# A graph attention layer on one core: rows of x for 63 gather tiles fetched in the prologue, their k and v made in the walk

## The chip, the cores and the metric

The kernel runs on one core of a Trainium2 chip. Times are device microseconds (us) of one execution. The kernel before was timed nine times: median 2628.71 us, from 2615.65 to 2638.81. The profile is one execution, recorded by the hardware profiler; it took 2623.65 us.

The engines are named as in the profile: PE is TensorE (matmuls and transposes), DVE is VectorE, ACT is ScalarE, POOL is GpSimd, which here issues the indirect DMAs, and SP is SyncE, which issues nearly all other DMAs.

## The reference

There are 12500 nodes with 256 features, and 200000 edges (src, dst), sorted by dst. The layer first normalizes and clips, then attends over each node's incoming edges with 8 heads of 32, and then adds, normalizes and adds the input:

```python
h = relu(layernorm(x))
q, k, v = h @ Wq + bq, h @ Wk + bk, h @ Wv + bv          # each 12500 x 256, 8 heads of 32
logits  = sum over d of q[dst] * k[src] / sqrt(32)       # edge x head
attn    = softmax of logits over the edges of one dst
out     = sum over the edges of a dst of attn * v[src], + h @ Wskip + bskip
y       = h + gelu(out)
result  = x + layernorm(y) * gamma + beta
```

All of it is in 32-bit floating point.

## The kernel before, in words

**Prologue (0 to about 243 us).** `project` goes over x in 98 blocks of 128 rows: it loads them, makes the row statistics (DVE), normalizes and clips (ACT, L218), transposes twice (PE, L138), multiplies by the 256 x 512 matrix of Wk and Wv (PE, L247), adds the bias (DVE, L250) and stores h in the DRAM table `h_tab` and k and v, 512 numbers a node, in `kv_tab`. In between stands `make_plan`, which works out on the chip which edges and nodes belong to which step: it loads the edges' dst and src (`load_edges`, L390 and L392), stores them shifted (`dst_p`, `src_p`), cuts them into steps with 16 small indirect DMAs (L472), and writes tables: `idx` (the gathers' row numbers), `d0_row` (first node of each window), `pen_tab` (penalties for the running maxima), `e_tab` (six rows of numbers from which 0/1 matrices are made; L649, L658). The scheduler lays plan and projection into each other on DVE, PE and POOL; on POOL the plan alone stands. `pieces` splits a bias into three bf16 parts, so that a 3-row matmul can add it in PSUM.

**Walk (about 245 to 2590 us).** The edges are cut into 8 streams (S), each of 66 steps of up to 3 tiles (K) of 128 edges. A step handles one tile of all eight streams three times. For each tile, `gather` (L1024) issues eight indirect DMAs on POOL, one for a stream, each of 128 rows of 512 numbers from `kv_tab`, into one of six buffers `kv`. A buffer comes free when `weigh` of its tile is done; gathers for step c+2 are issued during step c. The rest of a tile:

- `spread` (PE, L1062): the rows of q for the edges, as a product of a 0/1 matrix `to_e` with the window of queries `qw`, in PSUM `ps_qe`, two halves.
- `times` (DVE, L1071, two halves): multiplies k by q in place; `total` (DVE, L1078) sums over a head.
- `weigh` (DVE, L1129): multiplies v by the weights, giving `vw`; `add_up` (PE, L1148) sums it over edges by the 0/1 matrix `to_n`. ACT copies the sums out, and the last node's sums into the next step's first tile (L1163).

Once a step: `maxima` (two scans on DVE, L1099 and L1100, a subtraction, and Exp on ACT, L1103), `turn_back` (PE, L1111), `hot_n` (PE and ACT, L1050 and L1052), and for step c+2 `turn_windows` (PE L1000, ACT L1003: 192 node rows `hw` transposed, in two parts), `queries` (PE L1013 and L1017, ACT L1019) and `hot_e` four times (PE L1039, ACT L1041).

**Pairs.** From step 10 on, finished nodes are closed in pairs of 128-row blocks: pair m is fetched in step 10 + 39m/32 and worked on in the two steps after it, so four steps in six both start on a new pair (`pair`) and end an old one (`before`), one has only an old one and one only a new one. `turn` and `skip` (PE L822, L835, L839), `divisors`, `divide` (DVE L814, L816, L828), `add` (PE L844), `gelu` (ACT), `stats` (DVE L851 to L857), `root` (ACT L861), and a step later `factors` (DVE L865, L866), `normal` (ACT L871), `shifted` (PE L878, L881), `scale` (DVE L885, L887) and `store` (SP).

**Order.** In the walk each instruction goes through `keep`, which fixes the order of every engine to that of the program text; so an instruction that waits holds up all that stands behind it on its engine. The loop's body (L1233 to L1333) is that order. Relevant places: `times` of the step's last tile opens the body and the `spread` for it closes the middle of the body before; between the last `hot_e` and that `spread` PE has nothing else:

```python
                for i in range(1, S // 2):
                    hot_e(c + 2, i)
            for half in range(2):
                times(c + 1, 1, half)
                if tiles_of(c + 1) == K:
                    spread(c + 1, K - 1, half)
```

Tiles live in pools with a number of buffers: `hw` 2, `pen` 2, `hT` and `o` of a pair 2, and PSUM `ps_hot` 2, shared by all of `turn_windows`, `queries`, `hot_e`, `hot_n`, `turn`, `shifted` and a part of `add_up`. When all buffers of a name are in use, the next writer waits for the last reader.

Of the kernel before, what the change touches and what calls it, by code (L numbers as in the profile page):

```python
# [57 lines left out]
SURE = 50  # L58
PAD = 127.0
# [8 lines left out]
def gnn_kernel(ctx: ExitStack, tc: tile.TileContext, x, src, dst, Wq, bq, Wk, bk, Wv, bv,  # L68
# [22 lines left out]
    w_q = consts.tile([P, KC, HID], F32, name="w_q")  # L91

# [3 lines left out]
    b_s3 = consts.tile([3, 2, HID], BF16, name="b_s3")  # L96
    nc.vector.memset(one_row, 1.0)
# [12 lines left out]
    def pieces(b3, b, scale):  # L110

        with tc.tile_pool(name="pcs", bufs=1) as pool:
            left = pool.tile([3, 3, HID], F32, name="left")
            t = pool.tile([3, 3, HID], BF16, name="piece")
            own = pool.tile([3, 2], F32, name="piece_of")
            nc.gpsimd.iota(own, pattern=[[1, 2]], base=0, channel_multiplier=1,
                           allow_small_or_imprecise_dtypes=True)
            rows(left[:, 0, :], b)
            nc.vector.tensor_scalar(left[:, 0, :], left[:, 0, :], scale, None, op0=OP.mult)
            for i in range(3):  # L120
                nc.vector.tensor_copy(t[:, i, :], left[:, i, :])
                if i < 2:
                    nc.vector.tensor_tensor(left[:, i + 1, :], left[:, i, :], t[:, i, :],
                                            op=OP.subtract)
            nc.vector.tensor_scalar(own[:, 1:2], own[:, 0:1], 0.0, None, op0=OP.is_equal)
            nc.vector.tensor_scalar(left[:, 0, :], t[:, 0, :], own[:, 1:2], None, op0=OP.mult)
            for i in (1, 2):
                nc.vector.tensor_scalar(own[:, 1:2], own[:, 0:1], float(i), None,
                                        op0=OP.is_equal)
                nc.vector.scalar_tensor_tensor(left[:, 0, :], t[:, i, :], own[:, 1:2],  # L130
                                               left[:, 0, :], op0=OP.mult, op1=OP.add)
            for i in range(2):
                nc.vector.tensor_copy(b3[:, i, :], left[:, 0, :])
# [20 lines left out]
    def project():  # L154
# [12 lines left out]
        with tc.tile_pool(name="proj_c", bufs=1) as cpool, \  # L167
# [18 lines left out]
            w_kv = cpool.tile([P, KC, 2 * HID], F32, name="w_kv")  # L186
# [36 lines left out]
            for g, (b0, n) in enumerate(zip(starts, sizes)):  # L223

                if g > 1 and g + 1 < len(sizes):
                    ready[g + 1] = prepare(g + 1)
                if g == 4:
                    make_near(tc, near, near_n, lambda ins: behind(ins, last))
                if g == 3:
                    for ins in [rows(gam, gamma)] + \  # L230
                            [weights(t, w) for t, w in ((w_q, Wq), (w_s, Wskip))]:
                        behind(ins, products[-1])
                    qscale = 1.0 / math.sqrt(D)
                    nc.vector.tensor_scalar(w_q, w_q, qscale, None, op0=OP.mult)
                    pieces(b_q3, bq, qscale)
                    pieces(b_s3, bskip, 1.0)
                    pieces(b_o3, beta, 1.0)
                    zero = cpool.tile([WN, HID], F32, name="zero")
                    nc.vector.memset(zero, 0.0)
                    behind(nc.scalar.dma_start(h_tab[NP:, :], zero), products[-1])  # L240
                h = ready.pop(g)
                kvo = pool.tile([P, 6, KV], F32, name="kvo")[:, :n, :]
                for b in range(n):
                    hT, turned = transposed(pool, psum, h[:, b, :])
                    ps_kv = psum.tile([P, 2 * HID], F32, name="ps_kv", bufs=4)
                    for c in range(KC):
                        ins = nc.tensor.matmul(ps_kv, hT[:, c, :], w_kv[:, c, :], start=c == 0,  # L247
                                               stop=c == KC - 1)
                    products.append(ins)
                    nc.vector.tensor_tensor(kvo[:, b, :], ps_kv, b_kv, op=OP.add)  # L250
                for tab, t in ((h_tab, h), (kv_tab, kvo)):
                    nc.sync.dma_start(tab[b0 * P:(b0 + n) * P, :]
                                      .rearrange("(p b) d -> p b d", p=P), t)
                if g < 2:
                    ready[g + 1] = prepare(g + 1)
# [68 lines left out]
    pen_tab = dram.tile([NST, 2, S, CH + 1], F32, name="pen_tab")  # L324
    with tc.tile_pool(name="pln", bufs=1) as pool, tc.tile_pool(name="pln_e", bufs=1) as ep, \
            tc.tile_pool(name="pln_ps", bufs=1, space=PSUM) as psum:
        products = project()
        make_plan(tc, pool, ep, psum, src, dst, N, LEN, NST, SLACK, NT, dram, ident, flag,
                  idx, d0_row, slot_row, e_tab, pen_tab, products)
    fits = nc.values_load(flag[0:1, 0:1], min_val=0, max_val=1)  # L330
    many = nc.values_load(flag[0:1, 2:3], min_val=0, max_val=1)
    with tc.If(fits > 0) as branch:
# [3 lines left out]
                     gam, eps)  # L336
# [45 lines left out]
def load_edges(nc, pool, a, E, C, fill, name):  # L382
# [5 lines left out]
    for lo, hi in ((0, full // 16 * 16), (full // 16 * 16, full)):  # L388
        if lo < hi:
            nc.gpsimd.dma_start(t[lo:hi], a[lo * C:hi * C].rearrange("(p c) -> p c", c=C))  # L390
# [14 lines left out]

def make_plan(tc, pool, ep, psum, src, dst, N, LEN, NST, SLACK, NT, dram, ident, flag, idx, d0_row,
              slot_row, e_tab, pen_tab, products):
# [13 lines left out]
    nc.vector.memset(zero, 0)  # L421
    dst_i = load_edges(nc, ep, dst, E, C, N, "edges_i")
    nxt_i = load_next(nc, ep, dst, E, C, N)
    nc.gpsimd.dma_start(dst_p[0:1, :], zero)
    nc.gpsimd.dma_start(dst_p[1:, 0].rearrange("(p c) -> p c", c=C), dst_i)
    d = ep.tile([P, C + 1], F32, name="chk_d")
# [4 lines left out]
    src_i = load_edges(nc, ep, src, E, C, 0, "edges_i")  # L431
# [4 lines left out]
    hd = ep.tile([NST, S - 1, SLACK + 1], I32, name="hd")  # L436
    ld = ep.tile([NST, 1], I32, name="ld")
    nc.gpsimd.dma_start(hd, bass.AP(tensor=dst.tensor, offset=dst.offset + LEN - 1,
                                  ap=[[0, NST], [LEN, S - 1], [1, SLACK + 1]]))
    nc.gpsimd.dma_start(ld, bass.AP(tensor=dst.tensor, offset=dst.offset + E - 1,  # L440
                                  ap=[[0, NST], [1, 1]]))
# [28 lines left out]
    for t, tab in ((dch, dst_p), (sch, src_p)):  # L470
        for s in range(S):
            nc.gpsimd.indirect_dma_start(  # L472
                out=t[:, s, :CH], out_offset=None, in_=tab[:, :],
                in_offset=bass.IndirectOffsetOnAxis(ap=at_i[:, s:s + 1], axis=0))
    sf = pool.tile([NST, S, CH + 1], F32, name="sf")
# [174 lines left out]

    row(5, lambda t: nc.vector.tensor_tensor(t, dl, turn[:, :, None].to_broadcast([NST, S, CH]),
# [3 lines left out]
    ones = pool.tile([NST, S, CH], BF16, name="row_ones")  # L655
    nc.gpsimd.memset(ones, 1.0)
    for r in (3, 4):
        nc.gpsimd.dma_start(e_tab[:, r * S:(r + 1) * S, :], ones)  # L658
# [92 lines left out]
def walk_streams(tc, N, HID, NST, KL, many, ident, idx, d0_row, slot_row, near, near_n, e_tab, pen_tab, h_tab,  # L751
                 kv_tab, table, x, out, w_q, w_s, one_row, b_q3, b_s3, b_o3, gam, eps):
# [31 lines left out]
    class Pair:  # L784
# [7 lines left out]
        def places(self):  # L792
# [3 lines left out]
            self.o = self.pool.tile([P, 2, HID], F32, name="o")  # L796
# [3 lines left out]
            self.y = self.o  # L800
# [17 lines left out]
        def turn(self):  # L818
# [5 lines left out]
            self.hT = self.pool.tile([P, 2, KC, P], F32, name="hT")  # L824
            self.keep(nc.scalar.copy(self.hT, ps))  # L825

        def divide(self):
            self.keep(nc.vector.tensor_mul(  # L828
# [65 lines left out]
    class Last(Pair):  # L894
# [7 lines left out]
        def places(self):  # L902
# [5 lines left out]
            self.o = self.g = self.sums[:, :, HEADS:]  # L908
            self.y = self.x

# [15 lines left out]
    with ExitStack() as es:  # L926
# [51 lines left out]
        def penalties(c):  # L978

            g = step[c]  # L980
            g["pen"] = early.tile([P, CH + 1], F32, name="pen", bufs=2)
# [4 lines left out]
        def windows(c):  # L986

            hw = step[c]["hw"] = hold.tile([P, 3, HID], F32, name="hw")
# [32 lines left out]
        def gather(c, j):  # L1021
            t = gath.tile([P, S, KV], F32, name="kv")
            for s in range(S):
# [5 lines left out]
        def gather_next(c, j):  # L1029

            if c + 2 < NST and j < tiles_of(c + 2):
                gather(c + 2, j)

# [148 lines left out]
        penalties(1)  # L1182
        for c in range(2):
            for j in range(tiles_of(c)):
                gather(c, j)
            if c == 0:
                windows(1)
                prefetch(2)
        for i in range(S // 2):
            hot_e(0, i)  # L1190
        for c in range(2):
            for part in range(2):
                turn_windows(c, part)
                queries(c, part)
            if c == 0:
                windows(2)
# [36 lines left out]
        for c in range(NST - 1):  # L1233
# [8 lines left out]
            if c + 3 < NST:  # L1242
                windows(c + 3)
# [8 lines left out]
            if before:  # L1252
                before.factors()
                before.normal()
            if c + 2 < NST:
# [15 lines left out]
            if pair:  # L1271
                pair.turn()
                pair.divisors()
                pair.skip()
            for half in range(2):
# [5 lines left out]
            if pair:  # L1281
                table_of(AF.Gelu)
                pair.divide()
            if pair_next:
                pair_next.fetch()
            if before:
                before.store(1)
# [10 lines left out]
            if c + 2 < NST:  # L1298
# [3 lines left out]
                for i in range(1, S // 2):  # L1302
                    hot_e(c + 2, i)
            for half in range(2):
# [8 lines left out]
            if c + 2 < NST:  # L1313
                penalties(c + 2)
            if c + 3 < NST:
                prefetch(c + 3)
            if c == NST - 2:
# [3 lines left out]
                if pair_next:  # L1321
                    pair_next.turn()
                    pair_next.skip()
            if pair:
                table_of(AF.Sqrt)
                pair.stats()
                pair.root()
                table_of(AF.Exp)
# [436 lines left out]
```

## Time and profile before

| | |
|---|---|
| median of nine runs | 2628.71 us (2615.65 to 2638.81) |
| profiled execution: its time, its span | 2623.65 us, 2621.8 us |
| PE, DVE, ACT, POOL busy | 1969.8, 1920.3, 1080.0, 1842.4 us |
| mean granted PE clock | 0.831 of full speed |
| gathers L1024 | 1576, mean 1140 ns, from 245.6 to 2532.8 us |
| the walk, a step | 34.4 us without pairs (steps 0 to 9), 35.1 us on average with them |
| DMA moved | 597.84 MB, 228 GB/s |

How to read what follows: a row of the group list names the source line, the engine, the operation, the tiles it writes and reads, and how often; after the bar come the busy time and mean of one, and then the time that the engine idled just before these instructions and what ended it. "issue" is time in which nothing that the profile shows was waited for. A row of the list of waits gives the engine, the tile and line that waited, what it waited for, the sum in us, how often, and the longest. A row of a timeline gives the start and length in us and, in brackets, the idle time before it and its end. The clock is the share of TensorE's full speed that the chip granted.

### The profile page before, as it was taken

What the parts mean: (1) busy time and instruction counts of PE and PEld (TensorE: products, weight loads), DVE (VectorE), ACT (ScalarE), POOL (GpSimd) and SP (SyncE); (2) the same over time, 40 slices, a digit from 0 to 9 for tenths busy, and PEclk for the clock granted to TensorE, in tenths of its full rate; (3) what the DMA queues carried; (4) which work ended last, traced back from release to release, by engine and by line L of the source; (5) the groups of instructions that cost most, each with busy time, mean ns of one, the idle gap of its engine ahead of it and who ended that gap; (6) DMA issues with size and microseconds to landing.
All of it is one profiled execution on the core that took longest, in us unless ns stands there. A gap on an engine that the chain in (4) does not pass through costs nothing. (4 is left out here: it accounts for less than half of the span.)

```text
span 2621.8 us, 34668 instructions
## 1 busy us (share of the span) xinstructions
PE 1969.8 (75%) x10196; PEld 1140.2 (43%) x10196; DVE 1920.3 (73%) x2205; ACT 1080.0 (41%) x2583; POOL 1842.4 (70%) x1648
## 2 busy tenths in 40 slices
PE   7898666666777777777777777777777777777775
PEld 3443433333444444444444444444444444444443
DVE  8886766666777678777677777776877776867774
ACT  3431222233444444344354344444443444453433
POOL 2302777777777777777777777777777777777750
PEclk9998766777798888888788788888888788888877
DMA  7857777777787777877787787777777877777761
GB/s 276 292 229 231 227 208 209 214 220 219 237 242 227 227 236 234 238 236 229 224 242 232 233 245 232 234 240 217 238 244 226 243 239 218 239 229 226 225 210 50
DMA packets 275980, 597.84 MB, mean 228 GB/s; under 512 B 52295, under 2 KB 166164, under 8 KB 273600
## 3 DMA queue, kind: packets, MB, share of 16 engines
q0 software_dynamic: 128768, 423.23, 54.9%
q1 hardware_dynamic: 146482, 171.81, 20.0%
q8 instruction: 84, 1.38, 0.2%
q14 instruction: 116, 0.95, 0.1%
q10 hardware_dynamic: 530, 0.47, 0.1%
HBM read 512.83 MB, written 82.47 MB: 227 GB/s over the span
## 5 line engine op out<-in xcount | busy, mean ns | idle before, releaser
L1024 POOL DMA_INDIRECT kv<-kv_tab,idx x1576 | 1797.2, 1140 | 501.6 <-issue 450.7
L1071 DVE TENSOR_TENSOR kv<-ps_qe,kv 128x1024 f32<-128x1024 f32 x394 | 470.4, 1220 | 336.1 <-DMA kv<-kv_tab,idx 224.8
L1062 PE MATMUL ps_qe<-qw,to_e 64*128 64x256 f32 x3152 | 476.2, 438 | 127.1 <-DVE kv L1071 126.2
L1062 PEld LDWEIGHTS ps_qe<-qw,to_e 64*128 64x128 f32 x3152 | 339.1, 213 | 275.9 <-issue 138.7
L1078 DVE TENSOR_REDUCE L<-kv 128x64 f32<-128x2048 f32 x197 | 450.4, 2286 | 6.7
L1129 DVE TENSOR_TENSOR vw<-w,kv 128x2048 f32<-128x2048 f32 x197 | 450.1, 2285 | 5.6 <-ACT w L1114 5.6
L1148 PE MATMUL ps_a<-vw,to_n 128*32 128x264 f32 (+1 forms) x2344 | 258.0, 454 | 130.2 <-DVE vw L1129 109.9
L1019 ACT COPY qw<-ps_hot 128x256 f32<-128x256 f32 (+1 forms) x132 | 63.2, 479 | 654.7 <-PE ps_hot L1017 643.3
L1017 PE MATMUL ps_hot<-w_q,hwT 128*128 128x256 f32 x792 | 255.9, 469 | 1.0 <-ACT hwT L1003 0.8
L887 DVE TENSOR_TENSOR o<-sums,ps_hot 128x512 f32<-128x512 f32 x46 | 31.6, 688 | 268.8 <-PE ps_hot L881 268.5
L1017 PEld LDWEIGHTS ps_hot<-w_q,hwT 128*128 128x128 f32 x792 | 169.1, 229 | 85.2 <-issue 56.2
L1148 PEld LDWEIGHTS ps_a<-vw,to_n 128*32 128x32 f32 (+1 forms) x2344 | 99.9, 132 | 244.2 <-DVE vw L1129 142.8
L247 PE MATMUL ps_kv<-w_kv,hT 128*128 128x512 f32 x392 | 186.8, 620 | 21.5 <-ACT hT L140 20.5
L1003 ACT COPY hwT<-ps_hot 128x256 f32<-128x256 f32 (+1 forms) x132 | 62.3, 472 | 296.4 <-PE ps_hot L1000 290.5
L960 ACT ACT_TABLE_LOAD x138 | 177.1, 1283 | 2.4
L1148 PE MATMUL ps_hot<-vw,to_n 128*64 128x264 f32 x808 | 167.3, 574 | 2.3 <-DVE o L887 2.3
L1163 ACT COPY kv<-ps_a 1x264 f32<-1x264 f32 x388 | 142.9, 368 | 6.3
L1041 ACT ACTIVATE to_e<-ps_hot,ones 128x384 f32<-128x384 f32 x264 | 142.3, 582 | 6.9 <-PE ps_hot L1039 6.8
L844 PE MATMUL ps_a<-o,ident 128*128 128x256 f32 x184 | 73.7, 539 | 94.0 <-DVE o L828 94.0
L839 PE MATMUL ps_a<-w_s,hT 128*128 128x256 f32 x368 | 127.4, 506 | 12.6 <-ACT hT L825 9.6
L871 ACT ACTIVATE sums<-sums,nm,rstd 128x256 f32<-128x256 f32 x92 | 50.2, 593 | 207.0 <-DVE nm L866 207.0
L1039 PE MATMUL ps_hot<-et,near 48*128 48x384 bf16 x264 | 89.6, 340 | 42.3 <-ACT qw L1019 26.1
(282 smaller groups left out, 2195.7 us busy)
## 6 DMA issues: line engine op xcount, KB each, us to landing
kv<-kv_tab,idx POOLq DMA_INDIRECT x1576
kv_tab<-kvo SPq DMA_DIRECT2D x14, 1536.0 KB
hw<-h_tab SPq DMA_DIRECT2D x264, 64.0 KB
table<-sums_w SPq DMA_DIRECT2D x264, 61.9 KB
pen<-pen_tab SPq DMA_DIRECT2D x66, 192.5 KB
sums<-table SPq DMA_DIRECT2D x92, 132.0 KB
x_f<-in_x_dram SPq DMA_DIRECT2D x92, 128.0 KB
h<-h_tab SPq DMA_DIRECT2D x92, 128.0 KB
```

Source lines behind the costliest of these rows:

```text
L247: ins = nc.tensor.matmul(ps_kv, hT[:, c, :], w_kv[:, c, :], start=c == 0, stop=c == KC - 1)
L839: self.keep(nc.tensor.matmul(self.ps[:, b, :], self.hT[:, b, c, :], w_s[:, c, :], start=False, stop=False, skip_group_check=True))
L960: keep(nc.scalar.activation(dummy[:, 1:2], dummy[:, 0:1], function))
L1017: keep(nc.tensor.matmul(ps[:, b, :], g["hwT"][:, b, k, :], w_q[:, k, :], start=False, stop=k == KC - 1, skip_group_check=True))
L1024: nc.gpsimd.indirect_dma_start(out=t[:, s, :], out_offset=None, in_=kv_tab[:, :], in_offset=bass.IndirectOffsetOnAxis(ap=idx[:, s, j, c:c ...
L1041: keep(nc.scalar.activation(step[c]["to_e"][:, i, :], ps[:, :CH], AF.Relu, scale=-1.0, bias=ones))
L1062: keep(nc.tensor.matmul(ps[:, b, a, :], g["to_e"][r, 2 * half + a, j * P:(j + 1) * P], g["qw"][r, (half + a) * half, :], start=True, stop= ...
L1071: keep(nc.vector.tensor_tensor(k, g["qe", half].rearrange("p b a d -> p a b d"), k, op=OP.mult))
L1078: keep(nc.vector.tensor_reduce(g["L"][:, j, :].rearrange("p (s h) -> p s h", s=S), g["kv"][j][:, :, :HID].rearrange("p s (h d) -> p s h d" ...
L1129: keep(nc.vector.tensor_tensor(t[:, :, HEADS:].rearrange("p s (h d) -> p s h d", h=HEADS), wj[:, :, :, None].to_broadcast([P, S, HEADS, D] ...
L1148: keep(nc.tensor.matmul(ps[at:at + w, :], g["to_n"][:, j, i * P + at:i * P + at + w], g["vw"][j][:, s, :], start=j == 0, stop=j == tiles_o ...
L1163: keep(nc.scalar.copy(step[c + 1]["kv"][0][0:1, s, HID - HEADS:], ps[at:at + 1, :]))
```

## The change

The walk no longer gathers k and v for stream 0 in the last tile of steps 2 to 64 (63 tiles, `EARLY = 2`). Instead

- the prologue gathers, on POOL, the 128 x 256 rows of x of these edges' src nodes, three tiles to a buffer and three buffers, and SP stores them in order in a DRAM table `x_early`. The first 30 (`FIRST`) stand ahead of the load of the src edges, the other 33 behind the plan's 16 indirect DMAs. The loads `hd` and `ld` stand earlier, and the two constant rows of `e_tab` are written later, from the buffers of the other rows;
- the walk loads such a tile a few steps ahead (`early_fetch`, SP), makes its statistics (`early_stats`, DVE; `early_root`, ACT; `early_normal`, DVE and ACT), transposes it (`early_turn`, PE and ACT) and multiplies it by the weights of k and v with their bias (`early_project`, PE), from where ACT copies the result to the place in `kv` where the gather would have put it. `early_project` stands between the last `hot_e` and the `spread` of the step's last tile. The weights `w_kv` stay in SBUF for the walk, and the bias is split by two more `pieces`. Table loads for Sqrt and Exp now stand in every step that has such a tile, not only in those with a pair;
- for room in SBUF, `pen`, `hw`, `hT` and `o` have one buffer in the walk; so the penalties of step c+1 (instead of c+2) are loaded late in step c, the windows of step c+3 at the end of step c instead of at its start, the result of a pair is written over its x rows (`y` is `x`), and the second store of a pair stands before the next pair's fetch.

```diff
@@ project, gnn_kernel
+    w_kv = consts.tile([P, KC, 2 * HID], F32, name="w_kv")
+    b_kv3 = consts.tile([3, 2, HID], BF16, name="b_kv3")
...
+                    pieces(b_kv3, bk, 1.0, range(1))
+                    pieces(b_kv3, bv, 1.0, range(1, 2))
...
+                if g == 2:
+                    between(lambda ins: behind(ins, products[-1]))
@@ new
+def gather_early(nc, pool, x, at, x_early):
+    n, _, HID = x_early.shape
+    G = 3
+    gathers = []
+    for e in range(0, n, G):
+        m = min(G, n - e)
+        t = pool.tile([P, G, HID], F32, name="x_e", bufs=3)
+        for i in range(m):
+            gathers.append(nc.gpsimd.indirect_dma_start(
+                out=t[:, i, :], out_offset=None, in_=x[:, :],
+                in_offset=bass.IndirectOffsetOnAxis(ap=at[:, e + i:e + i + 1], axis=0)))
+        nc.sync.dma_start(x_early[e:e + m].rearrange("e p d -> p e d"), t[:, :m, :])
+    return gathers
@@ make_plan
+    hd = ep.tile([NST, S - 1, SLACK + 1], I32, name="hd")
...
+    gathers = early()
+    behind(gathers[0], ins)
...
-    src_i = load_edges(nc, ep, src, E, C, 0, "edges_i")
+    src_i = load_edges(nc, ep, src, E, C, 0, "edges_i", lambda ins: behind(ins, gathers[FIRST - 1]))
...
+    behind(gathers[FIRST], ins)
...
+    ones = pool.tile([NST, S, CH], BF16, name="row5", bufs=2)
+    nc.gpsimd.memset(ones, 1.0)
+    for r in (3, 4):
+        nc.gpsimd.dma_start(e_tab[:, r * S:(r + 1) * S, :], ones)
     row(5, lambda t: nc.vector.tensor_tensor(t, dl, turn[:, :, None].to_broadcast([NST, S, CH]),
@@ Pair
-            self.y = self.o
+            self.y = self.x
...
-            self.hT = self.pool.tile([P, 2, KC, P], F32, name="hT")
+            self.hT = self.pool.tile([P, 2, KC, P], F32, name="hT", bufs=1)
...
+            self.o = self.pool.tile([P, 2, HID], F32, name="o", bufs=1)
@@ walk_streams
-            g["pen"] = early.tile([P, CH + 1], F32, name="pen", bufs=2)
+            g["pen"] = early.tile([P, CH + 1], F32, name="pen", bufs=1)
...
-            hw = step[c]["hw"] = hold.tile([P, 3, HID], F32, name="hw")
+            hw = step[c]["hw"] = hold.tile([P, 3, HID], F32, name="hw", bufs=1)
...
-            for s in range(S):
+            for s in range(1 if is_early(c) and j == K - 1 else 0, S):
...
+        def is_early(c):
+            return EARLY <= c < NST - 1
+        def early_fetch(c):
+            if is_early(c):
+                step[c]["xe"] = hold.tile([P, HID], F32, name="xe")
+                keep(nc.sync.dma_start(step[c]["xe"], x_early[c - EARLY]))
+        def early_stats(c):
...
+            keep(nc.vector.bn_stats(st, g["xe"]))
+            keep(nc.vector.bn_aggr(g["mv"], st))
+        def early_root(c):
+            g = step[c]
+            keep(nc.scalar.activation(g["rs"][:, 0:1], g["mv"][:, 1:2], AF.Sqrt, bias=eps))
+        def early_normal(c):
+            g = step[c]
+            keep(nc.vector.reciprocal(g["rs"][:, 0:1], g["rs"][:, 0:1]))
+            keep(nc.vector.scalar_tensor_tensor(g["rs"][:, 1:2], g["mv"][:, 0:1], -1.0,
+                                                g["rs"][:, 0:1], op0=OP.mult, op1=OP.mult))
+            keep(nc.scalar.activation(g["xe"], g["xe"], AF.Relu, scale=g["rs"][:, 0:1],
+                                      bias=g["rs"][:, 1:2]))
+        def early_turn(c):
+            g = step[c]
+            ps = hot_ps.tile([P, 2, KC, P], F32, name="ps_hot")[:, 0]
+            for k in range(KC):
+                keep(nc.tensor.transpose(ps[:, k, :], g["xe"][:, k * P:(k + 1) * P], ident))
+            g["xT"] = hold.tile([P, KC, P], F32, name="xT_e", bufs=1)
+            keep(nc.scalar.copy(g["xT"], ps))
+        def early_project(c):
+            g = step[c]
+            ps = hot_ps.tile([P, 2 * HID], F32, name="ps_hot")
+            keep(nc.tensor.matmul(ps, one_row, b_kv3.rearrange("o b d -> o (b d)"), start=True,
+                                  stop=False, skip_group_check=True))
+            for k in range(KC):
+                keep(nc.tensor.matmul(ps, g["xT"][:, k, :], w_kv[:, k, :], start=False,
+                                      stop=k == KC - 1, skip_group_check=True))
+            keep(nc.scalar.copy(g["kv"][K - 1][:, 0, :], ps))
@@ the loop's body
-            if c + 3 < NST:
-                windows(c + 3)
             for half in range(2):
                 times(c, K - 1, half)
...
+            if is_early(c + 1):
+                early_normal(c + 1)
             if c + 2 < NST:
                 turn_windows(c + 2, 0)
...
                 pair.skip()
+            if is_early(c + 1):
+                early_turn(c + 1)
             for half in range(2):
                 times(c + 1, 0, half)
...
+            if before:
+                before.store(1)
             if pair_next:
                 pair_next.fetch()
-            if before:
-                before.store(1)
...
                     hot_e(c + 2, i)
+            if is_early(c + 1):
+                early_project(c + 1)
             for half in range(2):
                 times(c + 1, 1, half)
...
-            if c + 2 < NST:
-                penalties(c + 2)
+            penalties(c + 1)
             if c + 3 < NST:
                 prefetch(c + 3)
+                windows(c + 3)
+            early_fetch(c + 3)
...
+            if pair or is_early(c + 2):
+                table_of(AF.Sqrt)
             if pair:
-                table_of(AF.Sqrt)
                 pair.stats()
+            if is_early(c + 2):
+                early_stats(c + 2)
+            if pair:
                 pair.root()
+            if is_early(c + 2):
+                early_root(c + 2)
+            if pair or is_early(c + 2):
                 table_of(AF.Exp)
```

## The prediction

> **What bounds the kernel now.** The page first. GpSimd (POOL) is busy 70% of the span, and nearly all of it is one row, the gathers, whose idle time is almost only "issue", 0.30 us each:
>
> ```profile
> PE 1969.8 (75%) x10196; PEld 1140.2 (43%) x10196; DVE 1920.3 (73%) x2205; ACT 1080.0 (41%) x2583; POOL 1842.4 (70%) x1648
> L1024 POOL DMA_INDIRECT kv<-kv_tab,idx x1576 | 1797.2, 1140 | 501.6 <-issue 450.7
> L887 DVE TENSOR_TENSOR o<-sums,ps_hot 128x512 f32<-128x512 f32 x46 | 31.6, 688 | 268.8 <-PE ps_hot L881 268.5
> ```
>
> So POOL issues almost back to back from 245.6 to 2532.8 us. Does it set the time all along? VectorE's waits say. First the steps without pairs (282.5 to 625.6 us), then one full step of the pair phase (1713.4 to 1750.8), then another (1398.6 to 1432.1):
>
> ```profile
> DVE kv L1071 <- DMA kv<-kv_tab,idx: 110.3, 32, 6.6
> ...
> DVE o L887 <- PE ps_hot L881: 5.8, 1, 5.8
> DVE kv L1071 <- PE ps_qe L1062: 4.4, 1, 4.4
> ...
> DVE o L887 <- PE ps_hot L881: 6.1, 1, 6.1
> DVE kv L1071 <- PE ps_qe L1062: 0.3, 1, 0.3
> ```
>
> Without pairs VectorE waits only for gathered rows, 11 us of each 34.4 us step: POOL bounds. In full steps it waits for no gather at all: the loop runs through VectorE (28 us busy), the ACT and TensorE chain to L887 (5.8) and the q rows of the step's last tile, made by `spread` (0.3 or 4.4). I call a step with a new and an old pair F (37.4 or 33.5 us here), one with the old pair only E (30.2 at 1825.8), one with the new only B (31.9 at 1856.0). What makes the two F differ is TensorE's clock, seen in its timeline:
>
> ```profile
> 1725.33 2.00 PE L1062 MATMUL ps_qe<-qw,to_e 64*128 64x256 f32 x16
> 1730.98 2.08 PE L844 MATMUL ps_a<-o,ident 128*128 128x256 f32 x4 [3.66 <-DVE o L828]
> 1737.63 3.69 PE L1017 MATMUL ps_hot<-w_q,hwT 128*128 128x256 f32 x8
> 1742.47 0.32 PE L1039 MATMUL ps_hot<-et,near 48*128 48x384 bf16 x1 [0.16 <-ACT to_e L1041]
> 1742.48 1.82 PE L1062 MATMUL ps_qe<-qw,to_e 64*128 64x256 f32 x14
> ```
>
> ```profile
> 1416.40 1.13 PE L844 MATMUL ps_a<-o,ident 128*128 128x256 f32 x4 [1.25 <-DVE o L828]
> 1420.62 1.99 PE L1017 MATMUL ps_hot<-w_q,hwT 128*128 128x256 f32 x8
> 1423.77 0.32 PE L1039 MATMUL ps_hot<-et,near 48*128 48x384 bf16 x1 [0.16 <-ACT to_e L1041]
> 1423.78 2.04 PE L1062 MATMUL ps_qe<-qw,to_e 64*128 64x256 f32 x16
> ```
>
> After an idle gap of 3.66 us before L844 the matmuls run at half speed (L1017 x8: 3.69 us) and spread comes late; after 1.25 us they don't (1.99). In both, spread starts the moment the last `hot_e` is done: nothing waits in between.
>
> Third, how far POOL lags in cycles of six steps (four F, E, B), the first mixed, the second all slow; and three neighbouring gathers:
>
> ```profile
> 695.90:905.20 209.30, 153.59 (x888) 92.78 (x884) 158.11 (x157) 94.63 (x223) 165.41 (x145) 0.86 0.79 235
> 1676.10:1887.90 211.80, 164.08 (x888) 98.41 (x884) 157.80 (x158) 94.80 (x223) 164.68 (x146) 0.83 0.79 233
> ```
>
> ```profile
> 1714.30 0.96 POOL L1024 DMA_INDIRECT kv<-kv_tab,idx  x1 [0.30 <-issue]
> 1715.56 1.76 POOL L1024 DMA_INDIRECT kv<-kv_tab,idx  x1 [0.30 <-issue]
> 1717.63 0.95 POOL L1024 DMA_INDIRECT kv<-kv_tab,idx  x1 [0.30 <-issue]
> ```
>
> The columns are window, length, then busy time of TensorE, its weight load, VectorE, ScalarE and POOL, the clock, DMA share and GB/s. In the mixed cycle VectorE waits 13.5 us for gathers, so its chain alone is 196 us; in the slow cycle 0.5 us: chain 211.3, and POOL itself waits some 3 us. An undisturbed gather starts every 1.256 us; the stretched ones (232, 290 us in all) mostly end 0.83 us after a `weigh` (188) or the gamma multiply L885 (44).
>
> **The change, part by part.** The sum is made against the profiled execution, 2623.65 us (span 2621.8), 5.06 below the median of the nine runs.
>
> *63 gathers leave the walk.* Those stretches belong to VectorE instructions whose number stays, so a gather is worth 1.256 us: 79 us if POOL bounded everywhere. It does in steps 0 to 11: 12 x 1.256 = 15 us gained there (VectorE's additional 0.9 us a step lies in its 11 us wait).
>
> The Trainium skill, "SBUF — State Buffer", section "Who interferes with whom", has VectorE instructions with two SBUF operands share a port with GpSimd, yet says its probe saw no stall of descriptor generation. Here 188 of 197 weighs stretch a gather; by the page's probe the stretch would be the gathers' own, at 1.457 us each (mean plus issue), and the full gain 92 instead of 79 us.
>
> *The prologue takes them.* 63 x 1.256 = 79 us more on POOL, which is busy 45 of 245 us there. The first 30 (37.7 us) stand ahead of the src edge load (72.4 us, after 16.8 us idle), the other 33 (41.4 us) ahead of the d_d store (123.7). In the built order the plan's later pieces sit 9 to 10 projected blocks further back (gvu behind 65 blocks instead of 56, wide behind 70 instead of 60), at 2.217 us a block some 20 to 22 us; POOL arrives at them 27 to 29 us later by my count, so TensorE and VectorE wait some 7 us. The last e_tab row moves from behind 93 blocks to behind 98, the last: 6.5 us of plan after the projection's end. Sum +14. Ends: +6 (tail alone) and +30 (POOL's whole delay shows). Two more `pieces` and hd, ld earlier lie under the projection.
>
> *early_project before spread.* Bias matmul 0.38 (the row of L835's kind), two 128x512 products 1.85 (L247: four records of 0.46 at full clock), and some 0.55 until the PSUM buffer that hot_e just filled is free: 2.8 us between the last hot_e and spread, where today nothing waits. In F and B all of it is VectorE's; in E spread has some 1.8 us in hand, so 1.0. The ACT copy to kv (0.60) runs beside spread. The new bn_stats and bn_aggr (0.42 + 0.17) lie in the wait for spread.
>
> *early_normal, early_turn.* The Relu (0.59, as L218) stands on ACT between the pair's normal and the window copy, on the chain to exp and L887: +0.55 in F, +0.2 in E. The two small VectorE instructions (0.16 each) end before ACT reaches exp. The two transposes (0.45) delay spread of tile 1, in B about 0.4, and shorten the gap before L844 from 3.65 to 3.2 us. That remains slow: gaps of 3.24 us (at 714.8 and 994.7) were followed by half clock too.
>
> The Trainium skill, "TensorE: Matmul & The Clock Gate", Part 1, puts the drop to half rate behind an idle window of about 3.4 us. By that 3.2 us could keep the clock full, and the slow steps would gain their 4 us back; no row decides between 1.55 (full) and 3.24 before L844.
>
> *Single buffers.* hw: its load is issued after turn_windows' second part (1736.45), eight issues take about 4.9 us (0.6 each, an estimate from POOL's plain stores, L425), the rows are used at 1748.66; the cover is some 5 us, and if that went, TensorE would wait at most 4.9 + 2. pen: free after the scans (1716), used at 1750.8. y in x's tile: SP's next fetch waits for store(1), some 3 us (d_d's store took 3.3 to land, L503's wait), with hw's load behind it; still before 1736. hT and o are used once a step. Zero for these; the end is 2 us a step. Table loads of Sqrt and Exp come in every step now, on ACT after the last to_e, where it idles 7 us. SP issues 63 loads more; hidden.
>
> *Sum.* F +3.35 (2.8 + 0.55), E +1.2, B +3.3: 4 x 3.35 + 4.5 = 17.9 a cycle. Mixed: chain 196 + 17.9 = 213.9 against 209.5 now (POOL alone would be near 202): +0.7 a step. Slow: 211.8 + 17.9 = 229.7: +3.0 a step. 33 mixed steps (12 to 39, 46 to 50) +23; 18 slow ones (40 to 45, 51 to 62) +54; step 63 +3.4. In all 2623.65 - 15 + 14 + 80 = 2703 for an execution like the profiled one, and 2708 for a median like the one shown.
>
> **The rivals.** (1) POOL bounds after all: 2623.65 - 79 + 14 = 2559. It takes added chain below 7 us a cycle, thus slack of over 2 us before spread, and no slow cycle; against it, the 0.16 us gap in both timelines. The mixed cycles break even at 13.5 us, 2.5 per F. (2) The clock stays full, the gap being shorter: F 33.2 + 3.35, E 31.4, B 30 to 35, a cycle 207.6 to 212.6, 34.6 to 35.4 a step against 35.1, over 54 steps -27 to +16: 2596 to 2639. For it the fast F steps, against it that no two stand side by side. This and (1) are the other side. (3) The slow clock locks everywhere, as in 12 of 12 F steps of the slow cycles: 33 mixed steps at 38.3 instead of 35 cost 110 instead of 23: 2789. (4) Only the prologue as I fear: +30 instead of 14, 2718.
>
> **How the numbers follow.** The mixture with its bounds (prologue +6 to +30, single buffers to 2 us in some steps, half the PSUM wait) 2645 to 2765: 0.55, with (4) in it; (3) 0.17; (2) 0.16; (1) 0.12. I take 2708; 80% from 2600 to 2790, which leaves out (1) and the top of (3); the likeliest alone 2645 to 2765. 0.3% (8 us) is about what can be told from no change. Faster: (1) and most of (2), 0.22; same 0.04; slower 0.74.
>
> **What would show it.** Early steps at 33.1 us instead of 34.4; the first walk gather near 260; in F a wait of VectorE for spread of 3 to 7 us, no wait for gathers; early_project's matmuls directly ahead of spread; POOL waiting for buffers, thus idle beyond "issue". Wrong if VectorE still waits for gathers in F steps (1), if L1017 x8 stays 1.99 us throughout (2), or TensorE waits for hw.

## The result, and the profile after

The changed kernel takes 2718.71 us (median of ten runs, 2696.63 to 2734.84), the kernel before 2627.16 (31 runs): a ratio of 1.0343, with a 95% interval of 1.032 to 1.0367. The forecast was 2708, with 2600 to 2790 about it. The profiled execution has a span of 2711.6 us, 89.8 more than before. Busy times and the rows that answer to those of before, from the page of the changed kernel:

```profile
PE 2073.2 (76%) x10638; PEld 1164.6 (43%) x10638; DVE 1969.3 (73%) x2485; ACT 1241.3 (46%) x2915; POOL 1768.9 (65%) x1650
L1086 POOL DMA_INDIRECT kv<-kv_tab,idx x1513 | 1659.4, 1097 | 678.0 <-issue 591.0
L946 DVE TENSOR_TENSOR x_f<-sums,ps_hot 128x512 f32<-128x512 f32 x46 | 31.6, 687 | 275.0 <-PE ps_hot L940 274.8
```

POOL is no longer back to back: 63 gathers fewer, and yet more idle time. Line numbers differ: L903, L946, L1079, L1154, L1177 and L1186 of the changed kernel are L844, L887, L1017, L1039, L1062 and L1071 of the one before, and its L887 is the divide (L828 before). Where the 89.8 us lie is read from the first of the two scans of each step (L1099 before, L1214 after); step 63 ends with that scan of step 64:

| stretch | before | after | difference | forecast |
|---|---|---|---|---|
| start to the scan of step 0 | 282.5 | 328.8 | +46.3 | +14 |
| steps 0 to 9 | 343.1 | 332.6 | -10.5 | -13 |
| steps 10 to 63 | 1896.6 | 1953.3 | +56.7 | +78 |
| the rest | 99.6 | 96.9 | -2.7 | 0 |

The total was near by luck: the prologue came out 32 us above the forecast, steps 10 to 63 21 us below it. What VectorE waits for in steps 0 to 63 ("the walk" in all that follows) says what took the place of what; the first lines are the kernel before (282.5 to 2522.2 us):

```profile
DVE o L887 <- PE ps_hot L881: 261.6, 43, 7.7
DVE kv L1071 <- DMA kv<-kv_tab,idx: 204.8, 76, 7.4
DVE kv L1071 <- PE ps_qe L1062: 102.8, 42, 4.5
```

and these the changed one (328.8 to 2614.7 us):

```profile
DVE x_f L946 <- PE ps_hot L940: 267.8, 43, 7.6
DVE kv L1186 <- PE ps_qe L1177: 187.3, 54, 6.5
DVE kv L1186 <- DMA kv<-kv_tab,idx: 109.9, 46, 6.4
```

VectorE waits 94.9 us less for gathers, 84.5 us more for spread, 6.2 more for the chain to L946, and is itself busy 43.0 us longer (1691.3 instead of 1648.3). In the waits gained and lost nearly cancel; the walk is 46 us longer, about what VectorE is busy longer. A full step (1631 to 1671 us) on PE; rows are start, length, instruction and, in brackets, the wait:

```profile
1649.95 2.07 PE L903 MATMUL ps_a<-o,ident 128*128 128x256 f32 x4 [3.02 <-DVE o L887]
...
1659.54 0.32 PE L1154 MATMUL ps_hot<-et,near 48*128 48x384 bf16 x1 [0.16 <-ACT to_e L1156]
1660.05 0.37 PE L1142 MATMUL ps_hot<-b_kv,one_row 3*128 3x512 bf16 x1 [0.19 <-ACT to_e L1156]
1660.35 1.98 PE L1145 MATMUL ps_hot<-w_kv,xT_e 128*128 128x512 f32 x4
1662.26 2.00 PE L1177 MATMUL ps_qe<-qw,to_e 64*128 64x256 f32 x16
```

Between the last hot_e (1659.54) and spread (1662.26) lie 2.72 us, where the kernel before had 0.01; the median over all steps is the same 2.72. And PE still stands 3.02 us idle ahead of L903, as it did before ahead of L844 (3.66 in the step shown in the prediction).

In the prologue, POOL's rows show where the plan falls behind: the src load, at 72.40 in the kernel before, and the store of d_d, at 123.73 there; then VectorE's last kvo (the projection's last addition), which ended at 242.7 there:

```profile
103.31 1.18 POOL L402 DMA_DIRECT2D edges_i<-in_src_dram  x2
...
162.97 0.60 POOL L557 DMA_DIRECT2D d_d<-d_i  x1
...
276.09 0.68 DVE L258 TENSOR_TENSOR kvo<-ps_kv,b_kv 128x512 f32<-128x512 f32 x1
```

One thing is needed to read the runs below: on four of the six later occasions every kernel ran much slower (the kernel before took 3160, 3182, 3248 and 3346 us, and 2621 on the other two), in the walk, while the traces show the projection ending as early as usual ("the slower condition" below).

### The profile page after: what moved, and what is told of

Its sections match the earlier page's. It is cut to its first block, busy times and chain, and to the rows that moved or that the text cites. A ratio compares the mean times of both kernels' runs of the same rounds, so it can differ in the third digit from the quotient of the medians.

```text
span 2711.6 us, 36335 instructions
## 1 busy us (share of the span) xinstructions
PE 2073.2 (76%) x10638; PEld 1164.6 (43%) x10638; DVE 1969.3 (73%) x2485; ACT 1241.3 (46%) x2915; POOL 1768.9 (65%) x1650
## 5 line engine op out<-in xcount | busy, mean ns | idle before, releaser
L1086 POOL DMA_INDIRECT kv<-kv_tab,idx x1513 | 1659.4, 1097 | 678.0 <-issue 591.0
L1186 DVE TENSOR_TENSOR kv<-ps_qe,kv 128x1024 f32<-128x1024 f32 x394 | 467.1, 1219 | 332.4 <-PE ps_qe L1177 204.1
L1177 PE MATMUL ps_qe<-qw,to_e 64*128 64x256 f32 x3152 | 443.0, 423 | 48.7 <-DVE kv L1186 48.7
L1177 PEld LDWEIGHTS ps_qe<-qw,to_e 64*128 64x128 f32 x3152 | 314.9, 205 | 187.8 <-issue 81.6
L1263 PE MATMUL ps_a<-vw,to_n 128*32 128x264 f32 (+1 forms) x2344 | 243.0, 434 | 160.3 <-DVE vw L1244 111.7
L1079 PE MATMUL ps_hot<-w_q,hwT 128*128 128x256 f32 x792 | 245.0, 453 | 1.0 <-ACT hwT L1065 0.8
L946 DVE TENSOR_TENSOR x_f<-sums,ps_hot 128x512 f32<-128x512 f32 x46 | 31.6, 687 | 275.0 <-PE ps_hot L940 274.8
L255 PE MATMUL ps_kv<-w_kv,hT 128*128 128x512 f32 x392 | 194.5, 641 | 29.0 <-ACT hT L145 27.9
L1079 PEld LDWEIGHTS ps_hot<-w_q,hwT 128*128 128x128 f32 x792 | 162.3, 220 | 82.7 <-issue 54.7
L1263 PE MATMUL ps_hot<-vw,to_n 128*64 128x264 f32 x808 | 154.8, 538 | 2.3 <-DVE x_f L946 2.3
L903 PE MATMUL ps_a<-o,ident 128*128 128x256 f32 x184 | 69.0, 510 | 84.1 <-DVE o L887 84.1
L255 PEld LDWEIGHTS ps_kv<-w_kv,hT 128*128 128x128 f32 x392 | 75.0, 202 | 117.5 <-issue 76.2
L1145 PE MATMUL ps_hot<-w_kv,xT_e 128*128 128x512 f32 x252 | 125.0, 618 | 0.0
```

What stands on the lines that cost most here:

```text
L1079: keep(nc.tensor.matmul(ps[:, b, :], g["hwT"][:, b, k, :], w_q[:, k, :], start=False, stop=k == KC - 1, skip_group_check=True))
L1086: nc.gpsimd.indirect_dma_start(out=t[:, s, :], out_offset=None, in_=kv_tab[:, :], in_offset=bass.IndirectOffsetOnAxis(ap=idx[:, s, j, c:c ...
L1145: keep(nc.tensor.matmul(ps, g["xT"][:, k, :], w_kv[:, k, :], start=False, stop=k == KC - 1, skip_group_check=True))
L1177: keep(nc.tensor.matmul(ps[:, b, a, :], g["to_e"][r, 2 * half + a, j * P:(j + 1) * P], g["qw"][r, (half + a) * half, :], start=True, stop= ...
L1186: keep(nc.vector.tensor_tensor(k, g["qe", half].rearrange("p b a d -> p a b d"), k, op=OP.mult))
L1263: keep(nc.tensor.matmul(ps[at:at + w, :], g["to_n"][:, j, i * P + at:i * P + at + w], g["vw"][j][:, s, :], start=j == 0, stop=j == tiles_o ...
```

## Experiments: the walk

Theory A says that the walk loses by early_project's place, 2.7 us ahead of spread, and by the half clock behind the idle gap; the rivals are the single buffers (B) and the additional work on ACT and VectorE (D, H).

**The same work in the gap.** The only edit of the kernel called in_gap is early_project's place:

```diff
             if pair:
                 table_of(AF.Gelu)
                 pair.divide()
+            if is_early(c + 1):
+                early_project(c + 1)
...
                 pair.add()
...
                     hot_e(c + 2, i)
-            if is_early(c + 1):
-                early_project(c + 1)
```

> The changed kernel with early_project moved on every engine's order from behind the last hot_e to just before the pair's add (L903), where PE waits 3.0 to 3.4 us for the divide. Theory A: it costs the chain nothing there and fills the gap behind which the clock fell, so L1079 x8 takes 1.99 us nearly everywhere and full steps take 33.3 to 34.5 us: 2580 to 2630 us. Rival E (the gap is no room: the transposed rows come too late from ACT, so the add and all behind it move back): 2690 us or more.

> The same kernel as in the run named in_gap, where the kernel before itself took 3160 us and all engines stalled at random: early_project moved from behind the last hot_e to just before the pair's add (L903), where PE waits 3.0 to 3.4 us for the divide. Theory A: it costs the chain nothing there and fills the gap behind which the clock fell, so L1079 x8 takes 1.99 us nearly everywhere and full steps take 33.3 to 34.5 us: 2580 to 2630 us. Rival E (the gap is no room: the transposed rows come too late from ACT, so the add and all behind it move back): 2690 us or more.

> The kernel of in_gap once more: the changed kernel with early_project just before the pair's add. In gap_and_plan the pair phase was that of theory A; here the prologue and the clip are the changed kernel's. Theory A: L1079 x8 at 1.99 us nearly everywhere, full steps 33.3 to 35 us, the first scan at 329 us: 2600 to 2640 us, 20 to 45 us above gap_and_plan's 2587. Rival E: 2690 us or more.

> The kernel of in_gap once more, now that the kernel before takes 2620 us again: the changed kernel with nothing but early_project moved from behind the last hot_e to just before the pair's add. Theory A (of the changed kernel's 90 us, the walk's part is early_project ahead of spread, with the half clock that follows): first scan at 329 us, pair phase 33.5 to 34.2 us a step instead of 36.2, 2590 to 2620 us. Rival H (the clip on ACT's way to exp or the single buffers make much of it): pair phase 35 us a step or more, 2650 us or more.

All four fell in the slower condition, where the kernel before took 3160 to 3346 us: 3336.26, 3341.9, 3465.13 and 3494.45 us. The three ratios that were given are 1.0554 (1.041 to 1.0697), 1.0639 (1.0572 to 1.0706) and 1.0521 (1.0418 to 1.0624). The expected times are of the other condition and can't be held against these. What the traces do show is order: the median from the last hot_e to spread is 0.01 us again in all four, and the pair's add waits over 2.8 us for the divide in 1, 0, 0 and 0 steps, against 23 of the changed kernel.

**The same with the clip moved and another prologue.** In gap_and_plan the Relu of the early rows stands behind `weights` on ACT, off the way to exp; the prologue's part of the edit is below.

```diff
-            keep(nc.scalar.activation(g["xe"], g["xe"], AF.Relu, scale=g["rs"][:, 0:1],
-                                      bias=g["rs"][:, 1:2]))
...
             weights(c)
+            if is_early(c + 1):
+                early_clip(c + 1)
@@ the prologue
-FIRST = 30
+FIRST = 15
...
-    behind(gathers[FIRST], ins)
...
-    nc.gpsimd.dma_start(wide, bass.AP(tensor=gvu_d.tensor, offset=gvu_d.offset,
+    ins = nc.gpsimd.dma_start(wide, bass.AP(tensor=gvu_d.tensor, offset=gvu_d.offset,
...
+    behind(gathers[FIRST], ins)
```

> early_project in the gap before the pair's add (as in in_gap), the clip of the early rows on ACT behind weights instead of on the way to exp, and a prologue with 15 gathers ahead of the src load (instead of 30) and 48 behind the load of wide, with the bias of k and v split in one go instead of two. Theory A (PE's order ahead of spread and POOL's order in the plan are what the changed kernel loses by): the first scan near 300 us instead of 328.8 on a chip where the kernel before takes 2627 us, full steps 33.3 to 34.5 us: 2545 to 2600 us there, 0.97 to 0.99 of the kernel before. Rival F (whatever runs beside, k and v made in the walk cost more than the gathers): a ratio of 1.01 or more.

Measured: 2587.23 us against 2620.57 of the kernel before, a ratio of 0.9883 (0.986 to 0.9905). That is 1.2% less than the kernel before, clear of noise but under 2%, and well below the changed kernel's 2718.71, though its prologue (333.4 us to the first scan, not 300) was a miss. All of the gain is the walk's: 2150.9 us, against 2285.9 of the changed kernel and 2239.7 before. PE in a full step:

```profile
1151.46 0.39 PE L1146 MATMUL ps_hot<-b_kv,one_row 3*128 3x512 bf16 x1
1151.78 1.98 PE L1149 MATMUL ps_hot<-w_kv,xT_e 128*128 128x512 f32 x4
1154.97 1.13 PE L903 MATMUL ps_a<-o,ident 128*128 128x256 f32 x4 [1.21 <-DVE o L887]
...
1159.19 2.00 PE L1079 MATMUL ps_hot<-w_q,hwT 128*128 128x256 f32 x8
...
1162.34 0.32 PE L1158 MATMUL ps_hot<-et,near 48*128 48x384 bf16 x1 [0.16 <-issue]
1162.35 2.04 PE L1181 MATMUL ps_qe<-qw,to_e 64*128 64x256 f32 x16
```

Here the products end before the divide does, the add still waits for it (1.21 us), and the matmuls behind it run at full clock: the eight matmuls of L1079 in a row (the x8 form; L1017 before) take over 3 us in none of 64 rows, where they did in 13 of 64 before and 10 of 64 after the change. Full steps take 33.1 to 36.4 us and the waits are (333.4 to 2484.3 us)

```profile
DVE x_f L946 <- PE ps_hot L940: 259.1, 43, 7.0
DVE kv L1190 <- DMA kv<-kv_tab,idx: 89.8, 44, 6.3
DVE kv L1190 <- PE ps_qe L1181: 82.9, 44, 4.6
```

Of the 135 us by which this walk is shorter than the changed kernel's, the wait for spread gives 104.4, that for gathers 20.1 and that for the chain to L946, which the clip could touch, 8.7. Two edits stand in this walk, but they lie on different stretches of a step, so the traces can tell them apart. Cut at five marks, the 34 full steps (steps 12 to 63) take on average, in us:

| stretch of a full step | before | after | gap_and_plan |
|---|---|---|---|
| first scan to L946 (the clip lies on it) | 9.25 | 9.37 | 9.16 |
| to the pair's add, L903 | 8.68 | 8.65 | 9.11 |
| to the last hot_e (half clock shows here) | 9.60 | 9.08 | 7.33 |
| to spread (early_project's old place) | 0.01 | 2.72 | 0.01 |
| to the next first scan | 8.49 | 8.56 | 8.74 |
| sum | 36.03 | 38.39 | 34.36 |

Of the 4.03 us between the last two columns, the place gives 2.71 and the clock behind the gap 1.75; the stretch of the clip gives 0.21, and the other two lose 0.64. Part of that is the new place's price: in 11 of the 34 steps the products end after the divide and the add comes 1 to 2 us later. So the place of early_project, with the clock that follows from it, carries it. Rival F falls, and so does B, since pen, hw, hT and o have one buffer here too, and POOL, with 1667.1 us busy and 432.0 of issue, fills 2099 of the 2150.9 us. A kernel with the place alone moved was not measured in this condition.

**The kernels that leave a part out.** In plain_walk `is_early` is false in the walk; in no_matmul two ACT copies stand for the three matmuls:

```diff
-            return EARLY <= c < NST - 1
+            return False
```

```diff
-            ps = hot_ps.tile([P, 2 * HID], F32, name="ps_hot")
...
-            keep(nc.scalar.copy(g["kv"][K - 1][:, 0, :], ps))
+            for i in range(2):
+                keep(nc.scalar.copy(g["kv"][K - 1][:, 0, i * HID:(i + 1) * HID], g["xe"]))
```

> The changed kernel, but the walk gathers all 24 tiles a step again and makes no k and v; the prologue with its 63 gathers and the single buffers stay. Theory A (the walk loses by early_project ahead of spread, and single buffers cost nothing): the first gather of the walk near 287 us as in the changed kernel, about 41 us later than before, then the walk as before: 2665 to 2680 us, steps without pairs 34.4 us, pair phase 35.1 us a step. Rival B (single buffers hold up the walk): pair phase 36 us a step or more and waits of PE for hw, 2715 us or more.

> The kernel of plain_walk once more, since in that run the kernel before took 3160 us: the changed kernel, but the walk gathers all 24 tiles a step again and makes no k and v; the prologue with its 63 gathers and the single buffers stay. Theory A (single buffers cost nothing, the prologue 41 us): the first gather near 287 us, then the walk as before: 2660 to 2680 us, steps without pairs 34.4 us, pair phase 35.1 us a step. Rival B (single buffers hold up the walk): pair phase 36 us a step or more, 2715 us or more.

> The changed kernel without the three matmuls of early_project; ACT copies the clipped rows instead, so k and v of these tiles are left out. Theory A: the 2.7 us ahead of spread go, the chain falls below POOL's pace again, the pair phase goes from 36.2 to some 34.2 us a step: 2600 to 2640 us, with waits of VectorE for gathers back in full steps. Rival D (the step is set by ACT's or VectorE's additional work or the clock): 2690 us or more.

> The kernel of no_matmul once more: the changed kernel without the three matmuls of early_project; ACT copies the clipped rows instead, so k and v of these tiles are left out. Theory A: the 2.7 us ahead of spread go, the pair phase goes from 36.2 to some 34.2 us a step: 2600 to 2640 us, with waits of VectorE for gathers back in full steps. Rival D (the step is set by ACT's or VectorE's additional work or the clock): 2690 us or more.

Measured, all with the slower walk: plain_walk 3221.51 and 3378.42 us, ratios 1.0234 (1.0105 to 1.0363) and 1.0426 (1.0353 to 1.0498); no_matmul 3249.08 and 3415.4 us, ratios 1.026 (1.0091 to 1.0429) and 1.0513 (1.0443 to 1.0582). They decide nothing on the walk of the other condition. no_matmul's total wait for spread, 49 and 37 us, lies below that of the kernels here that have the matmuls (87 to 171), as A would have it; but plain_walk, which has none either, waits 112 and 128. In this condition in_gap is slower than plain_walk by 3.2 and 2.1 hundredths of the kernel before, and no better than no_prologue below, which has early_project in its old place (1.0554 and 1.0639 against 1.0668 and 1.0531); so the gain of gap_and_plan is shown for the usual condition alone.

## Experiments: the prologue

The prologue can be read in all runs: up to the last kvo, the four traces plain_walk, no_matmul_2, in_gap_2 and in_gap_4 end at 278.1, 274.8, 277.7 and 275.4 us, the changed kernel at 276.8.

**Without the 63 gathers.**

```diff
-    gathers = early()
-    behind(gathers[0], ins)
...
-                keep(nc.sync.dma_start(step[c]["xe"], x_early[c - EARLY]))
+                keep(nc.sync.dma_start(step[c]["xe"], x[c * P:(c + 1) * P, :]))
```

> The changed kernel without the prologue's part: no 63 gathers, no table of early rows; the walk loads other rows of x of the same size in their place, so its output is not the layer's. The two additional pieces of the bias stay. Theory A: the walk as in the changed kernel (pair phase 36.2 us a step), the first scan near 293 us instead of 328.8, of which 10 us are the pieces: 2680 to 2690 us. Rival C (the prologue is late by its VectorE work and the order of the plan, not by the gathers): 2705 us or more.

> The kernel of no_prologue once more: the changed kernel without the prologue's 63 gathers and table; the walk loads other rows of x of the same size in their place, so its output is not the layer's. The two additional pieces of the bias stay. Theory A: the walk as in the changed kernel (pair phase 36.2 us a step), the first scan near 293 us instead of 328.8, of which 10 us are the pieces: 2675 to 2690 us. Rival C (the prologue is late by its VectorE work, not by the gathers): 2705 us or more.

The times, 3354.69 and 3431.48 us (ratios 1.0668, 1.0557 to 1.0779, and 1.0531, 1.0441 to 1.062), belong to the slower walk. The last kvo of no_prologue:

```profile
251.14 0.68 DVE L258 TENSOR_TENSOR kvo<-ps_kv,b_kv 128x512 f32<-128x512 f32 x1
```

It ends at 251.8 us (252.0 in no_prologue_2): 9 us after the kernel before, 25 before the changed one. Of the 34 us by which the projection's end moved, 25 are thus the gathers' (with the working out of their row numbers, which the edit drops too) and 9 belong to the rest, which I had put at nothing: the two pieces more and the earlier loads, which no run separates. Rival C falls as the main cause. The src load, too, is already at 91.51 us without any gather (72.40 before, 103.31 with them).

**Gathers in other places.** gap_and_plan put 48 behind wide. The projection's middle came 20 us nearer (block 72's kvo at 198.5 instead of 218.7 us), but its end was lost:

```profile
DVE kvo L258 <- DMA kv_tab<-kvo: 25.6, 3, 17.5
```

The last stores of kv_tab were late. By the order of the program they share SP with the stores of the early rows, which wait for gathers; without those on SP, in plan_again, this wait is 5.0 us. So plan_again gives those stores to POOL, a group late, and spreads the gathers (30, 8, 10, 15) over the plan:

```diff
+        late.append((x_early[e:e + m].rearrange("e p d -> p e d"), t[:, :m, :]))
+        if len(late) > 1:
+            nc.gpsimd.dma_start(*late.pop(0))
...
+    behind(gathers[FIRST], ins)
...
+    behind(gathers[FIRST + 8], ins)
...
+    behind(gathers[FIRST + 18], ins)
```

> The walk of gap_and_plan with another prologue: 30 gathers ahead of the src load, 8 behind the store of src_p, 10 behind the load of d_row, 15 behind the load of wide; the tables of early rows are stored by POOL, one group late, so that no such store stands on SP ahead of the projection's stores (in gap_and_plan one held up the last stores of kv_tab, VectorE 17.5 us); the bias of k and v is split from the tile that the projection holds anyway, without a load. Theory A: the last kvo near 255 us (before 242.7, gap_and_plan 285.1), the first scan near 298 us, the walk as in gap_and_plan: 2545 to 2565 us where the kernel before takes 2620, a ratio of 0.971 to 0.979. Rival G (POOL's plan is late by the gathers wherever they stand): the last kvo at 270 us or more, 2575 us or more.

Measured: 2597.71 us against 2620.79, a ratio of 0.9911 (0.9877 to 0.9945). The expectation was missed and rival G is what came: the first scan at 347.8 us, the last kvo at 300.7. POOL waits for its own stores' data and brings d_d later than ever, and VectorE stands for it:

```profile
DVE df L551 <- DMA dch<-dst_p,at_i: 20.4, 1, 20.4
...
153.79 0.79 POOL L453 DMA_DIRECT2D x_early<-x_e  x1 [5.83 <-DMA x_e<-in_x_dram,rows_at]
...
185.90 0.62 POOL L562 DMA_DIRECT2D d_d<-d_i  x1
```

The walk, with 2150.3 us, repeats gap_and_plan's 2150.9 to 0.6 us behind a prologue 14 us longer; so the two parts add. No place that was tried makes the gathers of the prologue cheap: the three prologues that hold them reach the first scan 46 to 65 us later than before, and the gathers are 79 us of POOL's time.

## Why the prediction was right, point by point

- **The likeliest case came about**: a mixture of steps bound by the chain, VectorE waiting for spread and hardly for gathers in full steps (29.1 us over the pair phase, 94.4 before).
- **"F +3.35 (2.8 + 0.55)"**: the 2.8 us ahead of spread measured 2.72. The 0.55 of the clip did not show: the wait at L946 grew by 6.2 us in 43 steps, 0.14 each. VectorE's busy time grew by 43.0 us, 0.7 a step, of which I had taken all as covered; in full steps 0.28 of it shows (from spread to the next scan 8.29 us before, 8.57 after, medians). Full steps at full clock went from 33.1-33.8 to 36.2 us, +2.9.
- **"Steps without pairs -15"**: they take 33.1 us from step 1 to 9 (34.4 before), as said; over steps 0 to 9 the gain is 10.5 us, at 1.256 us a gather for nine steps 11.3.
- **"Slow: +3.0 a step", "33 mixed steps, 18 slow ones"**: this kept each step's clock as it was, and is the term of the walk that was mis-sized. The 18 slow steps grew by 27.2 us and not by 54, the 33 mixed ones by 32.1 and not by 23. Of the 12 full steps among the 18, the x8 form was at half clock in all before the change and is in 4 after it, and the stretch from the add to the last hot_e is 28 us shorter over the 12: that is the 27 us that are missing. In the whole walk the x8 form is at half clock in 10 rows instead of 13, the add in 17 instead of 23.
- **The gap "from 3.65 to 3.2 us. That remains slow"**: of 23 gaps of 3.02 to 3.44 us ahead of L903, 18 had half clock (the add takes 2.07 us, not 1.13) behind them. The Trainium skill, "TensorE: Matmul & The Clock Gate", Part 1, puts the drop at about 3.4 us of idling in windows that run freely: the rows have it behind 3.02 us too, so the length alone does not decide, and five gaps of 3.44 us were followed by a full-speed add. The granted clock that the traces record allows both: in each trace it changes only at marks that lie whole multiples of 3.413 us apart. Ahead of the adds of the two kernels 46 gaps are over 2.8 us: in the 41 with half clock behind them the gap covers 2.12 us or more of one such window, in the five others at most 1.96 of any. This is no limit for other places, where further idle time falls into the same window.
- **The prologue, "sum +14, ends +6 and +30"**: the step that failed. It is +46.3 to the first scan: the projection's end 34.1 (25 from the gathers, 9 from pieces and loads that I had laid "under the projection"), the tail behind it 7.3 (6.5 foreseen), and 4.9 from the first gather (287.0, not 260) to the first scan. The "some 7 us" of waiting was the mis-sized term: only the wait for wide was counted, and d_row alone cost 10.0 us, since d_d's store stood behind seven gathers.
- **Single buffers at zero**: right as far as it shows: the walk comes to POOL's pace with the same buffers, and no stretch of a full step but the named ones grew by over 0.3 us.

Rival 2 (full clock, 2596 to 2639) was the one that told where a faster kernel lay: with the products in the gap the clock stays full behind it and the walk comes to POOL's pace, 2150.9 us.

## What to carry to other kernels

Work taken off the engine that seems to bind is paid where it is put: look in a timeline for the spot on the target engine where it idles in every step waiting for somebody else, and put it there, not where its result is next needed. Here one spot cost 2.7 us in a full step and the other some 0.5 on average, with the same instructions. A stage that shows an engine a fifth busy is no free room for it: what counts is whose order the additional instructions enter, and what stands behind them.

## What the runs showed of the hardware that was not expected

- PE's idle gap had a second price, its clock, and filling it with useful matmuls repaid it: the x8 form at 1.99 or 2.00 us in all 64 rows of gap_and_plan. In the four in_gap traces, all in the slower condition, 6 to 9 of 64 rows were at half clock all the same; why is open.
- In the slower condition several engines stood still at once, for time that the profile gives to no engine and no queue of this core ("remote"): 202 to 465 us of VectorE's time and 541 to 909 of ACT's in each of those ten traces, most of it behind the last kvo, and none in the other four. In in_gap_2 VectorE and ACT both waited 6.7 us:

```profile
1537.46 0.96 DVE L1214 TENSOR_TENSOR_SCAN ps_x<-pen,ps_x 64x384 f32<-64x384 f32 x1 [6.65 <-remote]
...
1538.84 0.37 ACT L1065 COPY hwT<-ps_hot 128x256 f32<-128x256 f32 x1 [6.68 <-remote]
```

What caused it stays open.
